# Layer 2 of a two-layer cross-attention kernel: both halves' scores placed around the value products, with a third set of probabilities

## The chip, the core and the metric

The kernel runs on one core of a Trainium2 chip, as one program. The metric is the time of one execution on the device in microseconds (us). The core's engines work in parallel, each through its own queue in order: TensorE (PE in the profile; its weight loads are PEld), VectorE (DVE), ScalarE (ACT), GpSimd (POOL) and SyncE (SP), which only issues DMAs here. ScalarE's queue issues some DMAs as well (ACTq). They wait for one another by semaphores. PSUM holds what TensorE computes until VectorE or ScalarE has read it.

## What is computed

Two cross-attention layers follow each other over 16 batches of 256 positions and 320 channels, with 20 heads of 16 channels. A context of 256 tokens gives keys and values. The changed code is in the second layer; cut to what matters:

```python
scores_t = jnp.einsum('bhsd,bhtd->bhst', q, k_t) * attn_scale
probs_t = jax.nn.softmax(scores_t, axis=-1)
text_out = jnp.einsum('bhst,bhtd->bhsd', probs_t, v_t)
attn_scores = jnp.einsum('bhsd,bhnd->bhsn', q, k_ip) * attn_scale
qsem = jnp.einsum('bhst,bte->bhse', probs_t, text_ehs)
qsem = _l2norm(qsem)
sem = jnp.einsum('bhse,bne->bhsn', qsem, ip_n)
probs_ip = jax.nn.softmax(attn_scores + SEM_SCALE * sem, axis=-1) * spatial_mask
out = (text_out + probs_ip @ v_ip) @ W_out + b_out + residual
```

So each group of four heads needs scores, probabilities, the products of the probabilities with the values, and a quadratic form of the probabilities with the context's Gram matrix, which gives the norm of `qsem`.

## The kernel before

Matrix products that need full accuracy are made of a rounded high part and a low part of each operand. Layer 1 runs in slots 0 to 79 and layer 2 in slots 80 to 159, one slot for a group of four heads, five groups for a batch (`NS` = 80, `NG` = 5). Two more slots finish the last groups. The PE's order is the program's order; on the other engines a scheduler orders the instructions when the program is built, within the dependences and a few chains set by hand (`anchor`, `queued`). Between the parts of a slot, `fill` issues steps of other tasks whose due time has come: projections, keys, the Gram matrix, the image softmax, the output layer.

A slot `k` of layer 2 (`slot1`) consists of these parts:

- `both1(k, t)` for the two halves t = 0 and 1 of the tokens. It makes the transposed scores T of group k (four matmuls, 50 rows each, two row halves of the array at a time), then the scores S of group k + 2 (four matmuls of 48 rows), from which only the row maxima are taken. VectorE reduces S (line 797); ScalarE takes the exponential of T into the probabilities `P` (line 802, two instructions per half). T has two PSUM banks, S has one buffer of two banks.
- `attend1(k - 2)`: eight matmuls of probabilities with values into 32-column quarters of the array (line 843), and four with a constant `zone`, which put the sums `W` of the quadratic form beside them (line 845); `settle1` then transposes and divides on VectorE (lines 889 to 893). The profile counts each of these matmuls twice.
- `norm1(k - 1, u, n)`: seven full-array matmuls for each of two pairs of heads u, in two pieces of four and three (line 830). Each piece's result is multiplied by the rest of the probabilities on VectorE (line 833); then the two pieces are added (line 835, on GpSimd for u = 0 and on VectorE for u = 1). The results lie in PSUM banks X, of which there are three for everything.
- `rounded1(k, u)`: ScalarE rounds half the probabilities (line 820) and GpSimd subtracts that from the probabilities (line 821).
- `stacks(k + 4)`: DMAs that load the stacked queries and keys of a later group into a half of one of the pairs `qs[i]`, `ks[i]`. There are `NR` = 4 such pairs, all used whole in layer 1; in layer 2 they form a ring of eight halves.
- `maxima1(k + 2)`: the maxima are transposed (line 808), cast by ScalarE (line 810) and sent by two DMAs from ScalarE's queue (line 812) into the stack of queries.

The probabilities `P` are two tiles per group out of a ring of `NP` = 4, so two groups' worth.

The tasks that the prediction meets: key-mask products for the image keys (line 501) and a transpose of their scores (978) on VectorE; the keys' high and low parts (147 on ScalarE, 148 on VectorE); the attended rows of the output layer (952 on VectorE, 751 on ScalarE, 753 on VectorE); the values (470 on ScalarE); and the output layer's products (523).

Of the kernel before, what the change touches and what calls it, by code (L numbers as in the profile page):

```python
# [8 lines left out]
F32 = mybir.dt.float32  # L9
FR = mybir.dt.float32r  # L10
# [6 lines left out]
B = 16  # L17
S = 256
# [18 lines left out]
SIZES = dict(RAW=2, KST=2, NP=4, NR=4, CTA=2, CTB=2, WB=4, M=2)  # L37
NS = B * NG
# [3 lines left out]
def RAMP(t):  # L42
    return t if t < -5 or t > 3 else (t + 5) * 0.375
# [5 lines left out]
def xattn2(  # L49
# [28 lines left out]
    f = lambda ap: ap.bitcast(F32)  # L78
    mm = nc.tensor.matmul

    def dma(out, in_):
        nc.sync.dma_start(*(f(ap) if ap.dtype == FR else ap for ap in (out, in_)))
# [4 lines left out]
    sb = ctx.enter_context(tc.tile_pool(name="sb", bufs=2))  # L87

    def bank(tag="X"):
        return ps.tile([128, 512], F32, tag=tag, name=tag, bufs=BANKS[tag])  # L90

    def scores():

        return ps.tile([128, 1024], F32, tag="S", name="S", bufs=1).rearrange("p (h t) -> p h t", h=4)
# [4 lines left out]
    def buf(tag, shape, dtype=F32, bufs=1, name=None):  # L99
        if tag in ("wB", "wD", "vr", "raw"):  # L100
            return sb.tile(shape, dtype, tag=tag, name=name or tag, bufs=bufs)
        size = 1
        for d in shape[1:]:
            size *= d
        if tag not in slots:
            slots[tag] = [0, dtype] + [const_tile([128, max(size, words.get(tag, 0))], f"{tag}_{i}", dtype) for i in range(bufs)]
        n, kind, *ring = slots[tag]
        assert kind == dtype and len(ring) == bufs, tag
        slots[tag][0] += 1
        t = ring[n % bufs][: shape[0], :size]  # L110
        names = "abcd"[: len(shape) - 1]
        if len(names) > 1:
            t = t.rearrange(f"p ({' '.join(names)}) -> p {' '.join(names)}", **dict(zip(names, shape[1:])))
        return t

    def const_tile(shape, tag, dtype=F32):
        return const.tile(shape, dtype, tag=tag, name=tag)
# [23 lines left out]
    def anchor(inst):  # L141
        anchors[inst.ins.engine] = inst
        return inst
# [111 lines left out]
    wq, wo = [lambda s, k, m=slice(None): wqt[:, s, k, m]], []  # L255


    qs = [const_tile([128, 4, S], f"qs{i}", FR) for i in range(SIZES["NR"])]
    ks = [const_tile([128, 4, S], f"ks{i}", FR) for i in range(SIZES["NR"])]
    ind0 = buf("raw", [128, 512], bufs=SIZES["RAW"], name="ind0")[:2, :S]  # L260
    dma(ind0, ind0_d)
    ind0r = buf("mt", [8, S], FR, name="ind0r")[:2]
# [277 lines left out]
    def stack_rows(d):  # L540
        return d.rearrange("r (d h) t -> (r d) h t", h=HP)
# [65 lines left out]
    QK, P, W, R = {}, {}, {}, {}  # L607
# [20 lines left out]

    def stacks1(k):
        b, g = divmod(k - NS, NG)  # L630
        n = 2 * SIZES["NR"]
        i = ((NS - SIZES["NR"]) % SIZES["NR"]) * 2 + (k - NS) % n
        Q, K = QK[k] = [x[i // 2 % SIZES["NR"]][:, 2 * (i % 2) : 2 * (i % 2) + 2] for x in (qs, ks)]
        get("k1", b)
        qd = get("o1", b)[0]
        for u in range(2):
            rows = slice(64 * u, 64 * u + XROW)
            hs = slice(4 * g + u, 4 * g + u + 3, 2)
            if k - NS < n:
                dma(K[64 * u + XROW : 64 * u + KS1], w1["ind"])  # L640
            dma(K[rows], stack_rows(kd[1][b][:, :, 0])[:, hs])
            dma(Q[rows], stack_rows(qd)[:, hs])
# [41 lines left out]
    def attend0(k):  # L684
        b, g = divmod(k, NG)
        v, pv = get("v0", b), bank("P")
        for vt in range(3):
            values0(k, pv, v, vt)
        settle0(b, g, pv)
# [20 lines left out]
    def values0(k, pv, v, vt):  # L710
        t, o = ((0, 0), (0, S), (1, S))[vt]
        for s in range(4):
            h = V0W * (4 * (k % NG) + s)
            mm(  # L714
                pv[32 * s : 32 * s + 32, o : o + S],
                v[:, vt, h : h + 32],
                P[k, s // 2][:, t, s % 2],
                start=vt < 2,
                stop=vt != 1,
            )  # L720
# [56 lines left out]
    def both1(k, t):  # L777

        a = k + 2 < 2 * NS and QK[k + 2] 
        c = NS <= k < 2 * NS and QK[k]  # L780
        if a:
            if t == 0:
                maxes[k + 2] = buf("mn", [128, 4, 4], FR, bufs=2)[:, :2]
            sp = scores()
        if c:
            st = [bank("T").rearrange("p (h t) -> p h t", h=2) for u in range(2)]
            lo = (0, DUP)[t]
            for j in range(2):
                for u in range(2):
                    rows = slice(64 * u, 64 * u + KS1)  # L790
                    mm(st[u][:, j], c[1][rows, j, lo : lo + 128], c[0][rows, j], start=True, stop=True)  # L791
        if a:
            for j in range(2):
                for u in range(2):
                    rows = slice(64 * u, 64 * u + XROW)
                    mm(sp[:, 2 * u + j], a[0][rows, j, t * 128 : (t + 1) * 128], a[1][rows, j], start=True, stop=True)  # L796
            anchor(nc.vector.tensor_reduce(maxes[k + 2][:, t], sp[:, :, :T1], axis=AX.X, op=ALU.max))  # L797
        if c:
            for u in range(2):
                if t == 0:  # L800
                    P[k, u] = buf("P", [128, 2, 2, S], bufs=SIZES["NP"])
                anchor(nc.scalar.activation(P[k, u][:, t], st[u], AF.Exp, scale=SCALE))  # L802

    def maxima1(k):
# [43 lines left out]
    def slot1(k):  # L848
        last = k - 1 if NS < k <= 2 * NS else None
        mine = k < 2 * NS  # L850
        if k == NS:
            yield lambda: maxima(k + 1)
        elif k == NS + 1:
            yield lambda: attend0(k - 2)
        else:
            yield lambda: attend1(k - 2)
        yield lambda: both1(k, 0)
        if last:
            yield lambda: norm1(last, 0, 0)
        yield 0.33  # L860
        if last:
            yield lambda: norm1(last, 0, 1)
        yield lambda: both1(k, 1)
        if mine:
            yield lambda: rounded1(k, 0)
        yield lambda: stacks(k + LEAD)
        if last:
            yield lambda: norm1(last, 1, 0)
        yield 0.67
        if last:  # L870
            yield lambda: norm1(last, 1, 1)
        if mine:
            yield lambda: rounded1(k, 1)
        yield lambda: maxima(k + 2)
        yield 1.0
# [81 lines left out]
    def close0(b):  # L957

        def rows(p, hp):
            nc.vector.transpose(hp, hsn[:, p].rearrange("p f r d -> p (f r d)"))  # L960

        x1 = yield from finish(0, b, resid0.pop() if b == 0 else load(xT_d[b], "xc"), rows)
        dma(x1d[b].rearrange("(k p) t -> p k t", p=128), x1)
# [21 lines left out]
    def task(key, times, make, *needs):  # L985
        tasks[key] = [times, 0, make, needs, len(tasks)]
# [14 lines left out]
    def get(*key):  # L1001
        while key not in results:
            step(key)
        return results[key]
# [20 lines left out]
    def shifted(n, *times):  # L1025

        return [RAMP(n + t) for t in times]
# [10 lines left out]
    for c in range(B // 2):  # L1038
        n, k = 10 * c, [("k0", c)] if c else []
        task(("k0", c), FIRST["k0"] if c == 1 else shifted(n, -14.4, -13.3, -13, -12.4, -12, -10.8, -10.4, -9.8, -9.4, -8.8, -8.4), (lambda c=c: keys0(c)) if c else first_keys,  # L1040
             *([("w4", 0)] if c > 1 else []))
        task(("q0", 2 * c), shifted(n, -11.8, -11, -10, -9, -8), lambda b=2 * c: queries0(b))
        task(("q0", 2 * c + 1), shifted(n, -4.4, -4, -3, -2.8, -2), lambda b=2 * c + 1: queries0(b))
        task(("m0t", 2 * c), shifted(n, -7.4), lambda b=2 * c: tokens0(b), *k)
        task(("m0t", 2 * c + 1), shifted(n, -4.8), lambda b=2 * c + 1: tokens0(b), *k)
        task(("v0", 2 * c), shifted(n, -7, -5.4, -5), lambda b=2 * c: values0_(b), *k)
        task(("v0", 2 * c + 1), shifted(n, -4, -3.8, -3.4), lambda b=2 * c + 1: values0_(b), *k)
        for b, t in ((2 * c, (-7.4, -6.4, -6, -5.4, -5, -4.4, -3.4)), (2 * c + 1, (-2.4, -1.4, -1, -0.8, -0.4, 0, 1.2))):
            task(("s0", b), FIRST["s0"] if b == 1 else shifted(n, *t), lambda b=b: semantic0(b), ("q0", b), ("m0t", b))
            task(("c0", b), shifted(5 * b, *((5.6, 6, 6.6, 7.2, 7.6, 8.2) if b % 2 == 0 else (5.6, 6, 6.6, 7.2, 8.2, 9.2) if b < B - 1 else (6.33, 6.67, 7, 7.67, 8, 8.67))), lambda b=b: close0(b), ("w4", 0))  # L1050
    for b in range(B):
        n = NS + 5 * b
        task(("k1", b), shifted(n, -7, -6.67, -6.33, -5.67, -5, -4.67), lambda b=b: keys1(b), ("w2",), *([("t1", b - 1)] if b else []), *([("w4", 1)] if b > 2 else []))
# [162 lines left out]
```

## Time and profile before

| | |
|---|---|
| time, median of 3 runs | 1549.0 us (1548.74 to 1551.88) |
| the profiled execution's own time | 1545.33 us |
| its span, first to last instruction | 1543.5 us |
| granted TensorE clock | 0.992 |
| mean of one: reduction of S (797), exponential (802), rounding (820) | 1200, 598, 632 ns |
| mean of one: subtraction on GpSimd (821), multiplication (833) | 1321, 679 ns |

The profile gives for each engine its busy time, the groups of instructions, and for each group the idle time ahead of it with what ended it. A timeline row has the start in us from the span's start, the duration, the engine, the line of the kernel, the operation, what is written and read, the shape, and how many such instructions follow each other; in brackets stands the idle time before it and who ended it. Matmuls overlap, so what a part of TensorE's work costs is read from the start of one group to the start of the next. A view of one line lists for how long its engine sat idle before it and until which other line. In a row of windows, the columns are the stretch, its length, then busy time and count of instructions for PE, PEld, DVE, ACT and POOL, the clock, the share of DMA and its rate.

### The profile page before, as it was taken

How to read it: one execution, taken by the hardware profiler on the slowest of the kernel's cores; microseconds unless marked ns; L12 is line 12 of the kernel's file. 1: busy time of each engine (PE TensorE's matmuls, PEld its weight loads, DVE VectorE, ACT ScalarE, POOL GpSimd, SP SyncE). 2: the span in 40 equal slices, each digit the busy share in tenths (PEclk: the TensorE clock that was granted, in tenths of full speed). 3: DMA queues.
4: the chain of work that ended last, by engine and by line, in shares of the span. 5: the costliest groups of instructions: out<-in, count | busy, mean ns of one | idle time of the engine just before them, and what ended most of it. 6: DMA issues, size and time to landing. Idle time of an engine off the chain costs nothing.

```text
span 1543.5 us, 35120 instructions
## 1 busy us (share of the span) xinstructions
PE 1484.2 (96%) x12666; PEld 1202.0 (78%) x12666; DVE 1198.2 (78%) x2468; ACT 949.2 (61%) x2071; POOL 1165.0 (75%) x1178
## 2 busy tenths in 40 slices
PE   7899999999999998899999999999999999999997
PEld 6778888888888887777777787777777777777765
DVE  5457676777676779868888888888888888888796
ACT  5557676767676766755555655655555556556553
POOL 3459797979797867996777877877777777677685
PEclk9999999999999999999999999999999999999999
DMA  6756666656565565654433444344243434432301
GB/s 215 181 164 173 161 178 165 174 160 186 148 193 150 159 185 155 165 163 137 133 124 91 132 125 130 95 129 139 86 128 114 139 97 131 126 117 84 106 26 57
DMA packets 206426, 213.11 MB, mean 138 GB/s; under 512 B 29162, under 2 KB 190156, under 8 KB 206252
## 3 DMA queue, kind: packets, MB, share of 16 engines
q1 hardware_dynamic: 204512, 209.56, 47.3%
q8 instruction: 101, 1.65, 0.5%
q10 hardware_dynamic: 1740, 1.30, 0.3%
q14 instruction: 73, 0.60, 0.1%
HBM read 121.21 MB, written 88.18 MB: 136 GB/s over the span
## 4 chain that ended last, share of the span: by engine, by line
PE 85%; DVE 6%; DMA 3%; POOL 2%; issue 2%; ACT 2%; SPq 0%; ACTq 0%; POOLq 0%; DVEq 0%
PE X L205 23%; PE X L830 17%; PE X L523 11%; PE P L714 7%; PE S L653 6%; PE T L676 4%; PE T L791 4%; PE P L843 4%; PE P L845 3%; PE S L796 2%; PE X L951 1%; PE X L572 1%; DVE wt L835 1%; POOL P L682 1%; PE X L661 1%
## 5 line engine op out<-in xcount | busy, mean ns | idle before, releaser
L821 POOL TENSOR_TENSOR wt<-P,ctb 128x512 f32<-128x512 f32 x320 | 417.8, 1321 | 128.6 <-ACT ctb L820 128.4
L682 POOL TENSOR_TENSOR P<-P,rs 128x512 f32<-128x512 f32 x320 | 413.5, 1316 | 116.6 <-ACT P L679 116.6
L830 PE MATMUL X<-ctb,gm 128*128 128x512 f32 x1120 | 330.3, 413 | 0.9 <-DVE wt L833 0.9
L802 ACT ACTIVATE P<-T 128x512 f32<-128x512 f32 x320 | 174.1, 598 | 105.5 <-PE T L791 104.6
L679 ACT ACTIVATE P<-T 128x512 f32<-128x512 f32 x320 | 174.8, 593 | 97.6 <-PE T L676 73.5
L820 ACT ACTIVATE ctb<-P 128x512 fp32r<-128x512 f32 x320 | 195.4, 632 | 61.7 <-PE X L830 61.3
L830 PEld LDWEIGHTS X<-ctb,gm 128*128 128x128 f32 x1120 | 189.4, 188 | 46.6 <-DVE wt L833 1.5
L797 DVE TENSOR_REDUCE mn<-S 128x4 fp32r<-128x1008 f32 x160 | 192.0, 1200 | 0.2 <-PE S L796 0.2
L833 DVE TENSOR_TENSOR wt<-X,wt 128x512 f32<-128x512 f32 x240 | 161.8, 679 | 11.1 <-PE X L830 10.9
L655 DVE TENSOR_REDUCE mn<-S 128x4 fp32r<-128x716 f32 x160 | 142.5, 891 | 0.0
L714 PE MATMUL P<-P,vr 128*32 128x256 f32 x1920 | 124.6, 389 | 2.5 <-POOL P L682 1.2
L653 PE MATMUL S<-ks,qs 125*128 125x256 f32 x640 | 114.8, 302 | 4.2 <-DVE mn L655 4.2
L523 PE MATMUL X<-hq,wE 128*128 128x256 f32 x768 | 110.3, 287 | 6.8 <-ACT hq L512 4.0
L653 PEld LDWEIGHTS S<-ks,qs 125*128 125x128 f32 x640 | 86.5, 190 | 36.9 <-issue 30.4
L523 PEld LDWEIGHTS X<-hq,wE 128*128 128x128 f32 x768 | 102.8, 194 | 10.8 <-ACT hq L512 4.5
L523 PE MATMUL X<-ho,wF 128*128 128x256 f32 x768 | 108.8, 285 | 0.7 <-DVE ho L753 0.6
L205 PE MATMUL X<-cta,wA 128*128 128x252 f32 (+1 forms) x720 | 99.8, 284 | 8.5 <-ACT wA L147 5.7
L835 POOL TENSOR_TENSOR wt<-wt 128x512 f32<-128x512 f32 x80 | 103.6, 1296 | 2.5 <-DVE wt L833 2.5
L676 PE MATMUL T<-qs,ks 127*128 127x256 f32 x640 | 104.7, 286 | 0.0
L523 PEld LDWEIGHTS X<-ho,wF 128*128 128x128 f32 x768 | 100.8, 190 | 4.6 <-DVE ho L753 1.1
L205 PEld LDWEIGHTS X<-cta,wA 128*128 128x128 f32 x720 | 92.5, 192 | 11.5 <-ACT wA L147 5.9
L791 PEld LDWEIGHTS T<-qs,ks 50*128 50x128 f32 x640 | 47.7, 184 | 61.7 <-issue 33.2
(203 smaller groups left out, 3008.4 us busy)
## 6 DMA issues: line engine op xcount, KB each, us to landing
qd<-q SPq DMA_DIRECT2D x96, 384.0 KB
kd<-kst SPq DMA_DIRECT2D x73, 256.0 KB
rawc<-in_cT_dram SPq DMA_DIRECT2D x60, 256.0 KB
qs<-qd SPq DMA_DIRECT2D x80, 192.0 KB
ks<-kd SPq DMA_DIRECT2D x80, 192.0 KB
ks<-kd SPq DMA_DIRECT2D x160, 96.0 KB
qs<-qd SPq DMA_DIRECT2D x160, 96.0 KB
kd<-kst SPq DMA_DIRECT2D x21, 512.0 KB
```

Of the source, the lines that this page charges most:

```text
L205: last = mm(out, lhs(a, k), rhs(b, k), start=i == 0, stop=i == len(terms) - 1)
L523: mm(pp, w(s, k, slice(m * 128, (m + 1) * 128)), a[:, t], start=i == 0, stop=i == len(terms) - 1)
L653: mm(sp[:, h], Q[: XROW + T0, h, t * 128 : (t + 1) * 128], K[: XROW + T0, h], start=True, stop=True)
L676: mm(st[p][:, j], K[:KS0, 2 * p + j, t * 128 : (t + 1) * 128], Q[:KS0, 2 * p + j], start=True, stop=True)
L679: exp = anchor(nc.scalar.activation(pt, st[p], AF.Exp, scale=SCALE))
L682: anchor(nc.gpsimd.tensor_mul(pt, pt, rs[:, t : t + 1].to_broadcast([128, 2, S])))
L714: mm(pv[32 * s : 32 * s + 32, o : o + S], v[:, vt, h : h + 32], P[k, s // 2][:, t, s % 2], start=vt < 2, stop=vt != 1,)
L797: anchor(nc.vector.tensor_reduce(maxes[k + 2][:, t], sp[:, :, :T1], axis=AX.X, op=ALU.max))
L802: anchor(nc.scalar.activation(P[k, u][:, t], st[u], AF.Exp, scale=SCALE))
L820: nc.scalar.activation(R[k, u][:, t], P[k, u][:, t], AF.Copy, scale=0.5)
L821: anchor(nc.gpsimd.tensor_sub(W[k, u][:, t], P[k, u][:, t], f(R[k, u][:, t])))
L830: mm(yp, gm[:, gb], R[k, u][:, kt], start=i == 0, stop=i == len(blocks[n]) - 1)
```

## The change

In `slot1`, the two halves of `both1` are put around `attend1`, and all four pieces of `norm1` come after them. `attend0` of layer 1's last group runs one slot earlier, between the halves of slot 80. Since the first half of group k now writes probabilities before `attend1(k - 2)` has read its own, three sets of `P` are needed: the fourth pair of stacks becomes a pair of tiles in another pool (tags `qsl`, `ksl`), which layer 1 uses as stacks and layer 2 as the probabilities of every third group. The ring of stacks in layer 2 thus has six halves. The due times of the last batch's layer-1 output are earlier. The text has one line more above these functions, so that line 797 becomes 798 and so on.

```diff
-    qs = [const_tile([128, 4, S], f"qs{i}", FR) for i in range(SIZES["NR"])]
-    ks = [const_tile([128, 4, S], f"ks{i}", FR) for i in range(SIZES["NR"])]
+    last_stack = lambda shape, dtype, u: sb.tile(shape, dtype, tag=("qsl", "ksl")[u], name=("qsl", "ksl")[u], bufs=1)
+    qs = [const_tile([128, 4, S], f"qs{i}", FR) for i in range(SIZES["NR"] - 1)] + [last_stack([128, 4, S], FR, 0)]
+    ks = [const_tile([128, 4, S], f"ks{i}", FR) for i in range(SIZES["NR"] - 1)] + [last_stack([128, 4, S], FR, 1)]
...
-        n = 2 * SIZES["NR"]
-        i = ((NS - SIZES["NR"]) % SIZES["NR"]) * 2 + (k - NS) % n
-        Q, K = QK[k] = [x[i // 2 % SIZES["NR"]][:, 2 * (i % 2) : 2 * (i % 2) + 2] for x in (qs, ks)]
+        n = 2 * (SIZES["NR"] - 1)
+        i = (k - NS) % n
+        Q, K = QK[k] = [x[i // 2][:, 2 * (i % 2) : 2 * (i % 2) + 2] for x in (qs, ks)]
...
-                    P[k, u] = buf("P", [128, 2, 2, S], bufs=SIZES["NP"])
+                    P[k, u] = buf("P", [128, 2, 2, S], bufs=SIZES["NP"]) if (k - NS) % 3 else last_stack([128, 2, 2, S], F32, u)
...
         if k == NS:
             yield lambda: maxima(k + 1)
-        elif k == NS + 1:
-            yield lambda: attend0(k - 2)
-        else:
+        yield lambda: both1(k, 0)
+        if k == NS:
+            yield lambda: attend0(k - 1)
+        if k > NS + 1:
             yield lambda: attend1(k - 2)
-        yield lambda: both1(k, 0)
+        yield lambda: both1(k, 1)
         if last:
             yield lambda: norm1(last, 0, 0)
         yield 0.33
         if last:
             yield lambda: norm1(last, 0, 1)
-        yield lambda: both1(k, 1)
         if mine:
             yield lambda: rounded1(k, 0)
         yield lambda: stacks(k + LEAD)
```

More of the change, by code (lines that the diff above doesn't have):

```diff
@@ L1049, in xattn2 @@
             task(("s0", b), FIRST["s0"] if b == 1 else shifted(n, *t), lambda b=b: semantic0(b), ("q0", b), ("m0t", b))
-            task(("c0", b), shifted(5 * b, *((5.6, 6, 6.6, 7.2, 7.6, 8.2) if b % 2 == 0 else (5.6, 6, 6.6, 7.2, 8.2, 9.2) if b < B - 1 else (6.33, 6.67, 7, 7.67, 8, 8.67))), lambda b=b: close0(b), ("w4", 0))
+            task(("c0", b), shifted(5 * b, *((5.6, 6, 6.6, 7.2, 7.6, 8.2) if b % 2 == 0 else (5.6, 6, 6.6, 7.2, 8.2, 9.2) if b < B - 1 else (5.67, 6, 6.33, 7, 7.67, 8))), lambda b=b: close0(b), ("w4", 0))
     for b in range(B):
```

## The prediction, made before the changed kernel was run

> **What bounds the kernel now.** I read the page first, then the windows of layer 2, the waits of the zone products, and the timeline of one whole batch.
>
> ```profile
> span 1543.5 us, 35120 instructions
> PE 1484.2 (96%) x12666; PEld 1202.0 (78%) x12666; DVE 1198.2 (78%) x2468; ACT 949.2 (61%) x2071; POOL 1165.0 (75%) x1178
> ```
> ```profile
> 833.00:886.00 53.00, 52.47 (x430) 40.59 (x427) 44.70 (x84) 30.39 (x67) 40.02 (x44) 1.00 0.41 126
> ```
> ```profile
>   DVE wt L835: 23.5, 38
> ```
>
> TensorE has no slack: in one batch of layer 2 (five slots, 53 us) it is busy for 52.47 us, VectorE for 44.70, GpSimd for 40.02. The last row, from the view of line 845 over 780 to 1470 us, gives almost all the idle time that there is: the zone products wait 23.5 us for VectorE's sum (line 835). So time is won or lost on TensorE alone: by its own instructions, by changes of the array's shape, and by waits in its fixed order.
>
> I number a batch's slots 1 to 5 by their starts in the trace: 949.32, 959.30, 970.39, 979.77, 990.30. I count each slot 13 or 14 times: 16 batches, less the first two and the last, where the neighbouring work differs. Slot 2 shows the lengths:
>
> ```profile
> 959.30 1.07 PE L843 MATMUL P<-P,v1t 128*32 128x256 f32 x16
> 959.57 1.09 DVE L501 TENSOR_TENSOR kb<-kip,kmask 128x384 fp32r<-128x384 f32 x1
> 960.19 0.61 PE L845 MATMUL P<-wt,zone 128*32 128x256 f32 x8
> 960.73 0.50 PE L791 MATMUL T<-qs,ks 50*128 50x256 f32 x4
> 960.95 1.26 DVE L501 TENSOR_TENSOR kb<-kip,kmask 128x384 fp32r<-128x384 f32 x1
> 961.07 0.40 PE L796 MATMUL S<-ks,qs 48*128 48x256 f32 x4
> 961.27 1.09 ACT L802 ACTIVATE P<-T 128x512 f32<-128x512 f32 x2 [2.08 <-PE T L791]
> 961.40 1.20 PE L830 MATMUL X<-ctb,gm 128*128 128x512 f32 x4
> 963.06 1.20 DVE L797 TENSOR_REDUCE mn<-S 128x4 fp32r<-128x1008 f32 x1
> ...
> 964.21 0.86 PE L830 MATMUL X<-ctb,gm 128*128 128x512 f32 x3
> 964.99 0.51 PE L791 MATMUL T<-qs,ks 50*128 50x256 f32 x4
> 965.66 1.20 PE L830 MATMUL X<-ctb,gm 128*128 128x512 f32 x4
> 966.70 1.12 PE L523 MATMUL X<-ho,wF 128*128 128x256 f32 x8
> 967.66 0.86 PE L830 MATMUL X<-ctb,gm 128*128 128x512 f32 x3
> 968.36 0.28 PE L808 MATMUL X<-ident_r,mn 128*4 128x128 f32 x2
> ```
>
> From start to start: values 0.89, zone 0.54, T 0.34, S 0.33; front of a slot 2.10. The second T and S take 0.67 (964.99 to 965.66). Three norm products ahead of other full-array work take 0.70 (967.66 to 968.36) and ahead of T 0.78, so full to half rows costs 0.08. Four of them behind S take 1.04 where 4/3 of 0.70 is 0.93, so half rows to full costs 0.11. Both halves and the attend part thus take 2.10 + 0.67 + 0.08 + 0.11 = 2.96 us of an unstalled slot. The exponentials begin 0.54 after T and end 1.63 after it.
>
> **The change, part by part.** *Order.* TensorE gets the same instructions; T, S, attend, T, S, then full-array work. One full-to-rows and one rows-to-full change and the change into the value columns go; one into T's rows and one from rows to columns come. The last is not in the trace: 0 if the array takes it for nothing, 0.2 if it is twice the others; I take 0.10, the nearest rows' size. Unstalled, the front is 0.34 + 0.33 + 0.10 + 0.89 + 0.54 + 0.34 + 0.33 = 2.87, so 0.09 is saved per slot (from 0.19 saved to 0.01 lost).
>
> *New closeness.* S has one buffer, T two banks. The second S waits for the first reduction (line 797), the second T for the first two exponentials (802). They had the first half's norm products and a fill between them, 3.6 us in slot 2 (961.40 to 964.99); now only the 1.4 us of attend. From the slot's start T's second bank is wanted at about 2.3 and S at 2.54. So the reduction must start by 1.3 and the exponentials by 1.2. Whatever those engines do first at a slot's start is on the path. In the changed program as built, the first reduction stands in VectorE's queue behind these tails:
>
> *Slot 2.* Sum (835), both key-mask products (501) with a transpose between, then the reduction. The second 501 ends at 962.21, 2.91 after the start. Reduction to 4.11, second S to 4.44, norm products then, against 2.96: **+1.48**, 13 times, +19.2. Before, the reduction began even later (963.06), but the S that needs it came at 965.33 (964.99 + 0.34) and nothing showed.
>
> ```profile
> L501 DVE TENSOR_TENSOR kb<-kip,kmask x32: 535/1182/1422, 604.7 to 1387.4; 128x384 fp32r<-128x384 f32 x32
> ```
> A 501 takes 0.54 to 1.42 us. If both fell to 0.54 the slot would cost 1.2 less; if both took 1.42, 0.5 more. I keep the slot's own two: the subtractions beside them stay, slightly later. The Trainium skill, "SBUF — State Buffer", section "Who interferes with whom", has a VectorE instruction with two SBUF inputs contend with a GpSimd one that reads SBUF, the later one held until the first ends. By that rule at its full size each 501 could wait out a 1.3 us subtraction, 1.84 each and +1.3 for the slot; no row here is over 1.42, so the rows decide.
>
> *Slot 4.*
>
> ```profile
> 979.77 1.07 PE L843 MATMUL P<-P,v1t 128*32 128x256 f32 x16
> 980.66 0.59 PE L845 MATMUL P<-wt,zone 128*32 128x256 f32 x2
> 981.05 0.68 DVE L835 TENSOR_TENSOR wt<-wt,X 128x512 f32<-128x512 f32 x1
> 981.78 0.63 PE L845 MATMUL P<-wt,zone 128*32 128x256 f32 x6 [0.53 <-DVE wt L835]
> 982.35 0.50 PE L791 MATMUL T<-qs,ks 50*128 50x256 f32 x4
> 983.01 1.20 PE L830 MATMUL X<-ctb,gm 128*128 128x512 f32 x4
> ```
> The sum ends 1.96 after the start (the chain from the last norm product, which stays). The zone wait of 1.14 is now largely covered by T and S, but the reduction follows at 1.96 to 3.16; with 0.05 for the signal (981.73 to 981.78) the second S ends at 3.54. Before 3.24 + 0.86 = 4.10: **-0.56**, 14 times, -7.8.
>
> *Slot 5.*
>
> ```profile
> 990.30 1.07 PE L843 MATMUL P<-P,v1t 128*32 128x256 f32 x16
> 990.46 0.35 ACT L810 CAST mt<-X 4x256 fp32r<-4x256 f32 x1
> 990.83 1.29 ACTq L812 DMA_DIRECT2D qs<-mt  x2
> 991.74 0.42 DVE L952 TENSOR_TENSOR X<-hT,X 128x256 f32<-128x256 f32 x1
> 992.10 0.51 PE L791 MATMUL T<-qs,ks 50*128 50x256 f32 x4
> 992.19 0.37 ACT L751 CAST ho<-X 128x256 fp32r<-128x256 f32 x1 [1.12 <-DVE X L952]
> 992.63 1.09 ACT L802 ACTIVATE P<-T 128x512 f32<-128x512 f32 x2
> 992.77 1.21 PE L830 MATMUL X<-ctb,gm 128*128 128x512 f32 x4
> ```
> ScalarE issues the two maxima DMAs (1.29 us) and casts `ho` once VectorE has its sum (952, done 1.86 after the start). In the built order the exponentials stand behind both, as before, but T now runs at the start. If nothing shifts they run from 2.26 to 3.35; the second T ends at 3.66, S at 3.99. The first `ho` cast (0.37) now precedes the maxima's cast, which can push the DMAs to 2.18 and all of it to 4.30. Before 2.47 + 0.86 = 3.33: +0.66 to +0.97; I take **+0.80**, 14 times, +11.2. Were ScalarE not in the way, VectorE's order alone (952, then the reduction: 1.86 to 3.06, S to 3.44) gives +0.11; with another 0.4 from casts ahead, +1.4.
>
> *Slots 3 and 1.*
>
> ```profile
> 970.39 1.07 PE L843 MATMUL P<-P,v1t 128*32 128x256 f32 x16
> 970.50 0.53 ACT L470 ACTIVATE v1t<-X,tmask 128x320 f32<-128x320 f32 x1 [0.71 <-PE X L205]
> ```
> ```profile
> 949.32 1.07 PE L843 MATMUL P<-P,v1t 128*32 128x256 f32 x16
> 949.83 0.42 DVE L148 TENSOR_TENSOR kst<-X,kst 128x252 fp32r<-128x252 f32 x1 [0.77 <-ACT kst L147]
> ```
> Slot 3: the reduction now stands ahead of the small softmax steps, but ScalarE has a DMA issue (0.65) and the value copy (0.53) before the exponentials: they end near 2.3, so -0.09 to +0.3, taken **+0.10**, 13 times, +1.3. Slot 1: VectorE is free at 0.93, in time: **-0.09**, 13 times, -1.2.
>
> *GpSimd, queues, buffers.*
>
> ```profile
> 956.31 1.30 POOL L835 TENSOR_TENSOR wt<-wt 128x512 f32<-128x512 f32 x1
> ```
> In some slots GpSimd's sum now follows two subtractions, not one. It ended at 957.61 for a zone product at 960.19; 1.3 later, with the zone 0.77 later, is still in time. The norm products now run as seven in a row on three banks, but the fill before them and the multiplications (0.7 each) free a bank in time once the second reduction is done. Stack loads keep their place behind the fill, on SP's queue too; their ring of six halves is rewritten two slots after its last reader instead of four, covered by some 20 us. Four indicator DMAs fewer: nothing. The third set of probabilities is what allows the order and costs no instruction.
>
> *Sum.* 19.2 - 7.8 + 11.2 + 1.3 - 1.2 = +22.7 us in 67 of 80 groups; the first and last ones, waiting and unwaiting on the same engines, 0 (-4 to +4). Profiled execution 1545.3 + 22.7 = 1568; it lies 3.7 under the median of 1549.0, so **1572**.
>
> **The rivals.**
> *VectorE alone* (chance 0.15): ScalarE gets its exponentials out in time. Slots 3 and 5 fall to -0.09 and +0.11: 19.2 - 7.8 + 1.5 - 1.2 - 1.2 = +10.5, **1559**. For it: the exponentials start 0.54 after T in slots 2 and 5; against it: T was then 1.4 us into the slot.
>
> *Faster* (0.14): the zone wait is covered and the second half waits for nothing. It decides if the reduction starts by 1.3 in every slot. Slot 4 then gains 0.67 and slot 5 its wait of 0.36 (992.10 against 990.30 + 1.43), 14 times, 14.4, and 0.09 in 80 slots, 7.2: **1527**. For it: 23.5 us of waits are there. Against: the built order of slot 2.
>
> *Worse* (0.10): contention and ScalarE at their upper ends: 13 x 0.5 + 14 x 0.6 + 13 x 0.2 = 17.5 more, **1589**.
>
> *Only a move* (0.03): waits leave the zone products and appear at S in equal size, within 0.2% of 1549. Slot 2, which has no wait now, speaks against.
>
> **How the numbers follow.** The forecast has 0.58, with 1560 to 1585 of its own. Slower by over 0.2% (3 us, about what this kernel's measurement can tell) are it, VectorE alone and worse: 0.83; faster 0.14; same 0.03. The range 1553 to 1590 holds these slower cases with their bounds and leaves the faster one out.
>
> **What would show it.** Right: in slot 2 about 1.6 us of TensorE idle before the second S, released by line 797's reduction (one line further down in the changed text); in slot 5 about 1 us before the second T, released by the exponentials; the zone waits under 10 us in all; slots 2 and 5 longer, slot 4 shorter. Wrong: the second S starting within 2.6 us of the first T in slot 2, or 501 moved behind the reduction; a wait on GpSimd or on the X banks as the largest one.

## The result, and the profile after

The changed kernel takes 1557.1 us (median of 5 runs, 1554.9 to 1560.7) against 1549.0 for the kernel before on the same chip (5 runs, 1548.5 to 1551.9): ratio 1.0046, 95% interval 1.003 to 1.0061. It is slower, by 8 us, where 23 were forecast. Its profiled execution took 1554.9 us, 9.6 more than that of before; the terms of the prediction are held against these 9.6.

First the page of the changed kernel, then its windows over one batch (slots 5, 1, 2, 3, 4; columns as before: PE, PEld, DVE, ACT, POOL busy, clock, DMA share, GB/s), then what kept the engine idle ahead of the zone products from 780 to 1470 us (us, times).

```profile
span 1553.1 us, 35232 instructions
PE 1470.1 (95%) x12666; PEld 1209.7 (78%) x12666; DVE 1200.6 (77%) x2468; ACT 951.6 (61%) x2071; POOL 1167.4 (75%) x1178
```
```profile
944.16:998.35 54.19, 51.73 (x429) 41.06 (x428) 45.18 (x84) 30.65 (x67) 40.19 (x44) 1.00 0.38 117
```
```profile
  DVE wt L836: 4.6, 13
```

TensorE does the same 12666 instructions and is busy for 0.74 us less in a batch (51.73 against 52.47), yet the batch is 1.2 us longer. So the change saved TensorE time in its own work and in the zone wait (4.6 us against 23.5), and lost more in new waits. A view of one line adds the idle time of weight loads (PEld) and of matmuls (PE), which overlap, so the 23.5 counts part of the wait twice: the weight loads of the kernel before have 16.3 of it (first row below). The view of waits over 780 to 1470 us names the waits of each engine (engine, tile and line that waited, what released it; us in total, times, longest); the other two rows are the changed kernel's new ones:

```profile
PEld P L845 <- DVE wt L835: 16.3, 25, 1.3
```
```profile
PEld S L797 <- DVE mn L798: 19.5, 24, 1.4
PEld X L952 <- ACT mt L811: 17.1, 12, 1.4
```

The first of these two was forecast, the second was not. Slot by slot, I take the start of each slot's first norm product in both traces, and how far the changed kernel lags there. One batch:

| slot | before | after | lag | change in this slot |
|---|---|---|---|---|
| 1 | 951.43 | 958.43 | 7.00 | |
| 2 | 961.40 | 969.61 | 8.21 | +1.21 |
| 3 | 972.50 | 980.48 | 7.98 | -0.23 |
| 4 | 983.01 | 990.50 | 7.49 | -0.49 |
| 5 | 992.77 | 1001.13 | 8.36 | +0.87 |
| 1 | 1004.49 | 1012.63 | 8.14 | -0.22 |

The same over all 13 batches between 755 and 1446 us, beside the sum on record (which counts slots 4 and 5 once more):

| | slot 2 | slot 3 | slot 4 | slot 5 | slot 1 | first groups | last groups | sum |
|---|---|---|---|---|---|---|---|---|
| predicted | +19.2 | +1.3 | -7.8 | +11.2 | -1.2 | 0 | 0 | +22.7 |
| measured | +15.5 | -3.0 | -7.1 | +10.9 | -4.5 | +3.4 | -5.7 | +9.5 |

Slot 2 in the changed kernel's timeline (965.39 is its first T):

```profile
965.39 0.51 PE L792 MATMUL T<-qs,ks 50*128 50x256 f32 x4
965.71 0.59 DVE L502 TENSOR_TENSOR kb<-kip,kmask 128x384 fp32r<-128x384 f32 x1
966.31 2.82 POOL L822 TENSOR_TENSOR wt<-P,ctb 128x512 f32<-128x512 f32 x2
966.59 1.42 DVE L502 TENSOR_TENSOR kb<-kip,kmask 128x384 fp32r<-128x384 f32 x1
967.50 0.50 PE L792 MATMUL T<-qs,ks 50*128 50x256 f32 x4
967.93 1.20 DVE L798 TENSOR_REDUCE mn<-S 128x4 fp32r<-128x1008 f32 x1
969.18 0.50 PE L797 MATMUL S<-ks,qs 48*128 48x256 f32 x4 [1.18 <-DVE mn L798]
969.61 1.20 PE L831 MATMUL X<-ctb,gm 128*128 128x512 f32 x4
```

This is the forecast chain: both key-mask products, then the reduction, then the second S, released by it. Only the two products are shorter than assumed, 2.01 us together and not 2.35. The second of them lies beside a GpSimd subtraction (822). An unstalled front (slot 1) shows the lengths:

```profile
955.64 0.51 PE L792 MATMUL T<-qs,ks 50*128 50x256 f32 x4
955.99 0.41 PE L797 MATMUL S<-ks,qs 48*128 48x256 f32 x4
956.33 1.07 PE L844 MATMUL P<-P,v1t 128*32 128x256 f32 x16
957.22 0.61 PE L846 MATMUL P<-wt,zone 128*32 128x256 f32 x8
957.76 0.51 PE L792 MATMUL T<-qs,ks 50*128 50x256 f32 x4
958.43 1.19 PE L831 MATMUL X<-ctb,gm 128*128 128x512 f32 x4
```

The values start 0.34 after S, where S ahead of other work takes 0.33: going from rows to columns costs nothing that can be seen. The front is 2.79, where 2.87 was assumed and 2.96 stood before. And the end of slot 4, with slot 5's start:

```profile
941.13 1.05 PE L831 MATMUL X<-ctb,gm 128*128 128x512 f32 x3
941.81 1.15 ACT L821 ACTIVATE ctb<-P 128x512 fp32r<-128x512 f32 x2 [0.89 <-POOL wt L822]
942.87 0.35 ACT L752 CAST ho<-X 128x256 fp32r<-128x256 f32 x1
943.12 0.36 ACT L811 CAST mt<-X 4x256 fp32r<-4x256 f32 x1
943.53 0.30 PEld L952 LDWEIGHTS X<-rs,rs 128*128 128x128 f32 x2 [1.42 <-ACT mt L811]
943.53 0.70 PE L952 MATMUL X<-rs,rs 128*128 128x256 f32 x2 [1.23 <-DMA out_dram<-xc]
944.16 0.50 PE L792 MATMUL T<-qs,ks 50*128 50x256 f32 x4
945.13 0.60 ACT L803 ACTIVATE qsl<-T 128x512 f32<-128x512 f32 x1
```

The second image-value product (952) idles 1.23 us and starts at 943.53, 0.05 after the maxima's cast (811) ends at 943.48; its own row names an output DMA, but the row of its weight load names that cast, in all 12 batches that have the wait. As the changed program is built, this product's PSUM bank is the one that the maxima's small products have just left, in these 12 batches; in the program before it was one left by T. ScalarE comes to the cast late, behind two probability casts (821) and the output cast (752). The two probability casts had themselves waited 0.89 us. Their row names a GpSimd subtraction (822); but as the program is built they overwrite the tile that the slot's last norm product (831) reads, the subtractions of that tile are a slot older, and the casts start 0.67 to 0.69 us behind that product's start in all 12 batches. So the queue ahead of the maxima's cast is tied to the last norm product. Slot 5's front then has no stall: its exponentials run at 945.13, 0.97 after T.

### The profile page after: what moved, and what is told of

It is laid out like the page before. It is cut to its first block, busy times and chain, and to the rows that moved or that the text cites. A ratio compares the mean times of both kernels' runs of the same rounds, so it can differ in the third digit from the quotient of the medians.

```text
span 1553.1 us, 35232 instructions
## 1 busy us (share of the span) xinstructions
PE 1470.1 (95%) x12666; PEld 1209.7 (78%) x12666; DVE 1200.6 (77%) x2468; ACT 951.6 (61%) x2071; POOL 1167.4 (75%) x1178
## 4 chain that ended last, share of the span: by engine, by line
PE 74%; POOL 8%; DVE 8%; DMA 4%; ACT 3%; issue 2%; SPq 1%; ACTq 0%; POOLq 0%; DVEq 0%
PE X L205 21%; PE X L831 13%; PE X L524 10%; PE P L715 6%; PE S L654 5%; PE T L677 4%; POOL wt L822 3%; PE P L844 3%; PE T L792 3%; PE S L797 2%; POOL P L683 2%; DMA out_dram<-xc 2%; DVE mn L798 2%; DVE kb L502 2%; PE P L846 1%
## 5 line engine op out<-in xcount | busy, mean ns | idle before, releaser
L822 POOL TENSOR_TENSOR wt<-P,ctb 128x512 f32<-128x512 f32 x212 | 274.6, 1315 | 107.5 <-ACT ctb L821 107.5
L831 PE MATMUL X<-ctb,gm 128*128 128x512 f32 x1120 | 308.8, 405 | 0.0
L680 ACT ACTIVATE P<-T 128x512 f32<-128x512 f32 x320 | 174.7, 593 | 99.1 <-PE T L677 74.4
L831 PEld LDWEIGHTS X<-ctb,gm 128*128 128x128 f32 x1120 | 196.2, 189 | 41.0 <-issue 0.4
L821 ACT ACTIVATE ctb<-P 128x512 fp32r<-128x512 f32 x212 | 123.5, 625 | 57.1 <-PE X L831 48.0
L803 ACT ACTIVATE P<-T 128x512 f32<-128x512 f32 x212 | 114.5, 594 | 45.4 <-PE T L792 44.4
L822 POOL TENSOR_TENSOR wt<-qsl,ctb 128x512 f32<-128x512 f32 x54 | 70.9, 1324 | 50.8 <-ACT ctb L821 50.8
L726 DVE STREAM_TRANSPOSE nt<-P 128x512 f32<-128x512 f32 x80 | 57.1, 713 | 49.1 <-PE P L715 49.0
L655 DVE TENSOR_REDUCE mn<-S 128x4 fp32r<-128x308 f32 x160 | 74.8, 467 | 23.9 <-PE S L654 23.6
L654 PE MATMUL S<-ks,qs 125*128 125x256 f32 x480 | 86.3, 303 | 3.3 <-DVE mn L656 3.3
```

Of the source, the lines that this page charges most:

```text
L654: mm(sp[:, h], Q[: XROW + T0, h, t * 128 : (t + 1) * 128], K[: XROW + T0, h], start=True, stop=True)
L680: exp = anchor(nc.scalar.activation(pt, st[p], AF.Exp, scale=SCALE))
L821: nc.scalar.activation(R[k, u][:, t], P[k, u][:, t], AF.Copy, scale=0.5)
L822: anchor(nc.gpsimd.tensor_sub(W[k, u][:, t], P[k, u][:, t], f(R[k, u][:, t])))
L831: mm(yp, gm[:, gb], R[k, u][:, kt], start=i == 0, stop=i == len(blocks[n]) - 1)
```

## The experiments

All times are medians; ratios are to the kernel before, run on the same chip. Rows of experiment kernels carry their own line numbers, up to six higher. A few kernels below lost some 7 us twice in layer 1, which their edits do not touch, in some or most executions (the last section shows where, in the traces); where that is so, I compare slots of layer 2.

**The key mask out of slot 2's way.**

```diff
-        qh, qd = yield from queries(1, xs)
-
-        kb = image1(b)
-        yield
+        parts = queries(1, xs)
+        next(parts)
+        yield
+        next(parts)
+        kb = image1(b)
+        yield
+        qh, qd = yield from parts
+        yield
...
-            nc.vector.tensor_mul(
+            queued(nc.vector.tensor_mul(
```

> The changed kernel with one thing moved: the two products of the key mask (501 and 502 in the changed kernel's numbering) are issued one and a half slots earlier and behind slot 5's second reduction on VectorE, so that they no longer stand ahead of slot 2's first reduction. Theory (VectorE's queue is what stalls slot 2): slot 2's front falls from 4.19 to about 2.8 us and its second S follows its second T at once; 13 batches by 1.4 give -18, so 1557 becomes about 1539; slot 5 gets 1.1 to 2.5 us of VectorE before its first norm product is taken and may give up to 4 us of it back (1543). Rival (another wait stands right behind the reduction in slot 2, the exponentials or GpSimd's sum): the front of slot 2 stays above 3.5 us and the time above 1550.

Measured 1539.6, ratio 0.9944 (0.9928 to 0.996): faster than both kernels. Slot 2 in its timeline, and the 26 mask products from 780 to 1470 us (ns min/median/max):

```profile
960.25 0.50 PE L792 MATMUL T<-qs,ks 50*128 50x256 f32 x4
961.04 1.21 DVE L798 TENSOR_REDUCE mn<-S 128x4 fp32r<-128x1008 f32 x1
962.36 0.51 PE L792 MATMUL T<-qs,ks 50*128 50x256 f32 x4
963.03 0.96 PE L831 MATMUL X<-ctb,gm 128*128 128x512 f32 x3
```
```profile
L502 DVE TENSOR_TENSOR kb<-kip,kmask x26: 543/549/568, 785.1 to 1419.0; 128x384 fp32r<-128x384 f32 x26
```

The reduction starts 0.79 after T, the front is 2.78, and each slot 2 is 1.40 to 1.45 shorter, as the theory had it; the rival falls. Slot 5 gives nothing back: at their new place the products take 0.55 each. In the changed kernel the first of each pair takes 0.57 to 0.59 and the second 1.42, and all the second ones run beside a GpSimd subtraction; at the new place no GpSimd instruction runs beside them but one short copy.

**The second image-value product and its bank.** Three edits bear on it, in this order below: the first two products in the halves of one bank (e5); the output cast of the first product (`last_ho`) held behind the maxima's (f2, on e1_mask); the maxima ahead of the last norm product and of the casts that wait for it (f1, on e1_mask).

```diff
-            hp = bank()[:, :S]
+            if not (l and p == 1):
+                pair = bank()
+            hp = pair[:, S:] if l and p == 1 else pair[:, :S]
...
-        nc.scalar.copy(mt[:, 0], mp[:4, :S])
+        cast = nc.scalar.copy(mt[:, 0], mp[:4, :S])
+        if last_ho:
+            queued(last_ho.pop(), cast)
...
+        yield lambda: maxima(k + 2)
         if last:
             yield lambda: norm1(last, 1, 1)
         if mine:
             yield lambda: rounded1(k, 1)
-        yield lambda: maxima(k + 2)
```

> The changed kernel with the first two image-value products (952) in the two halves of one PSUM bank, so that the second no longer takes the bank which the maxima have just been cast out of. Theory (the bank is what holds the second product at the end of slot 4 for 1.2 to 1.4 us, and only that): the wait there goes, slot 5 starts 1.4 us earlier, and then the stall that the prediction had for slot 5 appears, ScalarE's two DMA issues and the casts ahead of the exponentials, +0.8 us in slot 5's front: -0.6 by 12 batches = -7, about 1550. Rival 1 (no stall in slot 5 even then): -1.4 by 12 = -17, about 1540. Rival 2 (the wait is ScalarE's late cast, whatever the bank): another instruction of slot 4 or 5 waits as long, 1557 within 2.

Measured 1589.6, ratio 1.0276 (1.0255 to 1.0298): all three expectations missed. The view of waits has a new row, for the same product:

```profile
PEld X L954 <- DVE ho L754: 28.4, 13, 2.2
```

The second half waited until VectorE had read the first half for the last time: in this program the wait goes by the bank, not by the columns. The Trainium skill, "PSUM — Partial Sum Buffer", section "PSUM bank collisions raise a hardware error", asks for that: guard PSUM by bank and quadrant, not by address. The run confirms that the bank's last reader sets this product's start: with VectorE as that reader the wait is up to 2.2 us.

> Base: e1_mask (1539.6). One edit more: ScalarE's output cast (752) of the first image-value product is held behind the maxima's cast of the same slot. Theory (the wait at the end of slot 4 is for the bank that the maxima's cast frees, and so as long as ScalarE's queue ahead of that cast): the second image-value product starts 0.35 us earlier, one cast's time: -4, about 1535. Rival (the output cast, now behind the two DMA issues of 1.3 us, comes between slot 5's exponentials and holds them by what was gained or more): 1540 or above.

Measured 1537.3, ratio 0.9937 (0.9921 to 0.9954). In the traces the product comes 0.26 earlier in each batch than in e1_mask, slot 5 keeps its length: the theory, with 0.26 in place of 0.35.

> Base: the changed kernel with the key-mask products moved as in e1_mask (1539.6). One edit more: the maxima's two small products, their cast and their two DMAs are issued ahead of the slot's last norm product and of the second pair of probability casts, not behind them. Theory (at the end of slot 4 the second image-value product waits for the maxima's cast because ScalarE comes to it after two probability casts and the output cast): the cast runs about 1 us earlier and the wait of 1.2 to 1.4 us goes; the DMA issues too are over before slot 5's exponentials, so nothing comes back there: -1.4 by 12 = -17, about 1523. Rival 1 (the stall goes to slot 5's front, as the prediction had it, 0.8 us): -7, about 1532. Rival 2 (the maxima, put ahead, delay the last norm product or the sums behind it as much): 1540 within 3.

Measured 1534.4 (four executions, 1528.3 to 1552.1; the longest is the one in the trace, with the loss in layer 1, and the ratio is without it), ratio 0.9904 (0.9879 to 0.9929). Slot 4 falls from 11.43 to 9.93 us, slot 5 grows from 11.48 to 12.20: net -0.8 per batch, rival 1 in size. Its timeline at that place:

```profile
954.04 0.36 ACT L811 CAST mt<-X 4x256 fp32r<-4x256 f32 x1 [0.71 <-PE X L809]
954.60 0.59 PE L952 MATMUL X<-rs,rs 128*128 128x256 f32 x2
955.12 0.50 PE L792 MATMUL T<-qs,ks 50*128 50x256 f32 x4
956.43 0.58 ACT L803 ACTIVATE qsl<-T 128x512 f32<-128x512 f32 x1
956.83 1.19 DVE L798 TENSOR_REDUCE mn<-S 128x4 fp32r<-128x1008 f32 x1
957.52 0.50 PE L792 MATMUL T<-qs,ks 50*128 50x256 f32 x4
958.08 0.50 PE L797 MATMUL S<-ks,qs 48*128 48x256 f32 x4
```

The bank, still the maxima's, is free in time. Now slot 5 waits at its front, 0.6 us, and two things are late there: ScalarE's exponentials and VectorE's reduction.

**What makes slot 5 late.** One more edit each: the maxima's DMAs issued by SyncE (g1), the second pair of probability casts issued in the next slot behind its first exponentials (g2), both (g3).

```diff
-            nc.scalar.dma_start(
+            nc.sync.dma_start(
...
-        if mine:
-            yield lambda: rounded1(k, 1)
         yield 1.0
...
         yield lambda: both1(k, 0)
+        if last:
+            yield lambda: rounded1(last, 1)
```

> Base: f1_max_first (1533 to 1534), in which slot 5's front is 0.6 us longer than an undisturbed one. One edit more: the maxima's two DMAs are issued by SyncE instead of ScalarE. Theory (the DMA issues, 0.63 us each on ScalarE, are what is late ahead of slot 5's exponentials): the stall shrinks by up to the one issue that still stands behind the output cast there, 0.3 to 0.6 by 13 = -4 to -8, about 1527. Rival (what is late are the probability casts and the output cast that waits for VectorE): within 2 of 1533.

> Base: f1_max_first (1533 to 1534). One edit more: the second pair of probability casts of a slot, with its two GpSimd differences, is issued in the next slot, behind the exponentials of that slot's first half. Theory (those two casts of 0.55 us stand ahead of slot 5's exponentials and make the second T late): slot 5's front falls from 3.39 to about 2.8: -0.6 by 13 = -8, about 1526. Rival (GpSimd then gets its differences 2 us later, in every slot, and the products with the zone or the norm products of the slot wait for it): 1540 or above.

> Base: g2_late_round, and the maxima's DMAs issued by SyncE as in g1_max_first_sp. Theory (both stand ahead of the exponentials, and their costs add): 2 to 8 us below g2_late_round. Rival (only one of the two was on the path): within 2 us of the lower of g1_max_first_sp and g2_late_round, or of both.

Measured 1547.9, 1546.3 and 1547.0, ratios 0.9996 (0.997 to 1.0022), 0.9992 (0.9968 to 1.0015) and 1.0002 (0.999 to 1.0014). g1's profiled execution, without the loss in layer 1, took 1533.1, g3's, with it, 1550.8, and most executions of all three lie nearer the second, so these medians decide nothing for or against the theories. In the profiled slots, slot 4 lasts 9.92 in each and slot 5 lasts 12.30, 12.08 and 12.28, against f1_max_first's 9.93 and 12.20. From g3's timeline of slot 5:

```profile
954.86 0.50 PE L792 MATMUL T<-qs,ks 50*128 50x256 f32 x4
955.69 0.59 ACT L803 ACTIVATE qsl<-T 128x512 f32<-128x512 f32 x1
955.71 0.42 DVE L953 TENSOR_TENSOR X<-hT,X 128x256 f32<-128x256 f32 x1
956.04 0.68 DVE L836 TENSOR_TENSOR wt<-wt,X 128x512 f32<-128x512 f32 x1
956.64 1.20 DVE L798 TENSOR_REDUCE mn<-S 128x4 fp32r<-128x1008 f32 x1
957.89 0.50 PE L797 MATMUL S<-ks,qs 48*128 48x256 f32 x4
```

The exponentials start 0.83 after T, 0.48 earlier than in f1_max_first, and the slot is no shorter: the second S still waits for the reduction, which VectorE starts 1.78 after T, behind the image values' sum (953) and the zone sum (836). So taking ScalarE's work away gains nothing, and the trace names VectorE; no run moved its two sums.

**The norm product between the halves.** The first edit is to the changed kernel, the second run adds the DMAs on SyncE.

```diff
-        yield lambda: both1(k, 1)
         if last:
             yield lambda: norm1(last, 0, 0)
+        yield lambda: both1(k, 1)
```

> The changed kernel with one part of the order undone: the first norm product stands between the two halves' scores again, behind the values, and not behind the second half. Theory (the front's length is set by the reduction's time and by the array's switches): the product's 1.0 us covers most of slot 2's wait for the reduction (from 1.33 to about 0.3 us), the fronts without a stall go from 2.78 back to about 2.96; here the second image-value product has another bank, so the 1.2 us at the end of slot 4 go too: -13 for slot 2, +11 for the switches, -7 to -17 for the bank: 1540 to 1550. Rival (which of the two stands last does not matter, the changed kernel loses by the values' late start): 1557 within 3.

> Base: e3_norm_between (1560.7), where the second image-value product has another bank and does not wait, and slot 5 is 2.2 us longer than in the changed kernel. One edit more: the maxima's two DMAs are issued by SyncE, not by ScalarE. Theory (what the prediction had for slot 5: two DMA issues of 0.65 us and the output cast stand ahead of the exponentials on ScalarE): the exponentials of slot 5 start up to 1.3 us earlier, the late first S and zone products of slot 5 go, and the probability casts behind them come earlier: -1.2 to -2 by 13 = -15 to -25, about 1541. Rival (SyncE waits in its queue for loads, so the maxima rows come late and the scores behind them wait): 1560 or above. Rival 2 (slot 5 is held by the casts and sums behind the second half, not by the DMAs): 1555 to 1562.

Measured 1560.7 and 1560.7, ratios 1.0088 (1.0067 to 1.011) and 1.009 (1.0073 to 1.0107): 3.6 above the changed kernel and so nearer e3's rival, though its slots move as the theory has it. Slots 1 and 3 grow by 0.2, the two changes of shape come back; slot 2 falls from 12.31 to 11.31; slot 4, where the bank is another, falls from 11.43 to 9.85; and slot 5 grows from 11.48 to 13.73, in e3 and f4 alike. Two rows of e3's waits make up most of it: the first S and a norm product in slot 5.

```profile
PEld X L831 <- DVE wt L834: 16.6, 12, 1.4
PEld S L797 <- ACT mt L811: 6.8, 13, 0.5
```

So where the second product does not wait, slot 5 does; f4's rival 2 holds: moving the DMAs off ScalarE brings slot 5's exponentials from 2.41 after its first T to 0.67 and saves nothing. (1560.7 is also at the edge of f4's first rival, late maxima rows, but no wait of TensorE for these DMAs stands in its view.)

**What is not the order's.**

> Everything of the change but the order of layer 2's groups: the fourth stack pair as third set of probabilities, the ring of six half stacks and the last batch's due times, with the old order of slots. Theory (those parts cost nothing by themselves, and all of the +8 us is the order's): 1549 within 3 us of the kernel before. Rival (the smaller ring of stacks holds loads up, or the third set of probabilities frees ScalarE earlier): over 3 us away from it, upwards for the ring, downwards for the set.

Measured 1551.6, ratio 1.0014 (0.9998 to 1.003): the steady part of layer 2 is that of before, 53.13 against 53.23 us per batch, so the smaller ring and the third set of probabilities cost nothing there. But layer 2 starts late, as in the changed kernel: its first norm product comes 5.6 us later than in the kernel before, the changed kernel's 4.9. f3_start moves the last layer-1 group's values back into layer 2's second slot (on e1), h1_old_due gives the changed kernel the old due times, h2_new_due gives the kernel before the new ones (the diff shows f3's edit and h2's; h1's is h2's reversed; h2's lines are cut to the part that changes).

```diff
-        if k == NS:
-            yield lambda: attend0(k - 1)
+        if k == NS + 1:
+            yield lambda: attend0(k - 2)
...
-else (6.33, 6.67, 7, 7.67, 8, 8.67)
+else (5.67, 6, 6.33, 7, 7.67, 8)
```

> Base: e1_mask (1539.6). One edit more: the last layer-1 group's values stand in layer 2's second slot again, between that slot's two halves, and not in the first slot. Theory (layer 2's start lost 4.9 us because nothing stands between the second slot's two halves, so the second half waits 2.9 us for VectorE, which itself waits for the mask's DMA): the values cover about 0.9 us of products and the wait falls by as much or more: -1 to -4, about 1537. Rival (VectorE gets the transpose and the sums of that group in the very slot where it is late): 1540 or above.

> The changed kernel with one part undone: the last batch's layer-1 output projection keeps its old due times. The changed kernel's first norm product of layer 2's third slot comes 4.9 us later than in the kernel before, and e4_old_order, with the old order of slots, has the same delay (5.6). Theory (the delay is the due times': the earlier projection pieces stand ahead of the last layer-1 group on VectorE and ScalarE): it goes, about 1557 - 4.9 = 1552. Rival 1 (it is the ring of six half stacks or the third set of probabilities): 1557 within 2, the delay stays. Rival 2 (the earlier due times pay for themselves later, by an earlier load of batch 15): slower than 1557.

> The kernel before with the last batch's new due times alone. Theory (the due times alone bring the delay of 5 us at the start of layer 2): 1553 to 1554. Rival (the delay comes from the ring or the third set of probabilities): 1548 to 1549, as before.

f3_start took 1542.4, ratio 0.9962 (0.9945 to 0.9978), not better than e1_mask: the rival. h2_new_due took 1549.1, ratio 1.0013 (1.0001 to 1.0025). The first zone products of layer 2 in the kernel before, in h2_new_due and in h1_old_due:

```profile
706.99 0.59 PE L845 MATMUL P<-wt,zone 128*32 128x256 f32 x2
```
```profile
701.29 3.19 PE L205 MATMUL X<-wC,cta 128*128 128x320 f32 x12 [2.76 <-DVE tmp L731]
713.00 0.61 PE L845 MATMUL P<-wt,zone 128*32 128x256 f32 x8
```
```profile
709.95 0.61 PE L846 MATMUL P<-wt,zone 128*32 128x256 f32 x8
```

The due times alone bring a start 6.0 us late, 2.8 of them one fill product that waits for VectorE's last layer-1 values. In the changed kernel they make the start 3.2 us later (713.19 against 709.95) and the end 3.4 us shorter; the profiled spans are equal, 1553.1 and 1553.7. So the late start was the due times', as both theories said, but their times are off: h2_new_due was to take 1553 to 1554 and is nearer the rival's 1548 to 1549, and h1_old_due, which was to fall to 1552, came out as its rival 2 said, slower than 1557. In the changed kernel the due times give the start back at the end. (h1_old_due's median is 1567.2, ratio 1.0115 (1.0084 to 1.0147): the profiled execution took 1555.5, the other three over 1565, and no profile shows why.)

> e1_mask (1539.6) with the last batch's old due times. Theory (the two parts are separate: the key mask's place costs slot 2 its 1.4 us per batch, the due times the start): 1535 to 1540, by what h1_old_due shows at the start. Rival (one depends on the other through the banks' placement): outside of that.

> f2_cast_first (1537.3: the key mask moved, the output cast behind the maxima's cast) with the last batch's old due times, to see whether the three corrections add up: 1537 less what h1_old_due gains at the start, 1532 to 1537, and so 12 to 17 below the kernel before. Rival (the corrections take from each other): 1540 or above.

Measured 1550.8, ratio 1.0015 (0.9992 to 1.0038), and 1547.4, ratio 1.0001 (0.9989 to 1.0013): both above what the theories said. Layer 2's steady batches are those of e1_mask and f2_cast_first (52.78 against 52.81, and 52.48 against 52.52 us); h4's profiled execution lost 15 us in layer 1, h3's had no such loss and took 1534.4, 13 and more below its others. Whether the corrections add up in a whole execution these two leave open.

## Why the prediction was right and wrong

The direction was right and the size was not: +22.7 us on record, +9.5 in the profiled executions (8 in the medians). What failed is the sum. Its largest mis-sized terms are those of slots 3 and 1: on record +0.1 us together, measured -7.5 (the switch from rows to columns, priced at 0.10 us, measured 0.01; ScalarE's work in slot 3, priced at 0.19, held nothing up). Slot 2 was right in mechanism and 3.7 us too dear, and slot 5's step was wrong in mechanism, with the right size by luck.

- **TensorE bounds the kernel, and the order decides by its waits.** Right: same instructions, a longer batch, and e4_old_order without the order has the old batch. The 23.5 us of zone waits, the case for *Faster*, were nearer 16, as said above.
- **Slot 2, +1.48 by the key mask ahead of the reduction.** Right in mechanism, shown by e1_mask; the size was 1.20. The two products took 2.01 us and not 2.35 (-0.34), which is nearly all by which the reduction comes earlier (2.54 after the first T and not 2.91); their lengths were taken over from the slot of before, where GpSimd's subtractions ran beside both, and now one runs beside the second alone.
- **Slot 4, -0.56.** Right: -0.54. The zone wait is covered, the reduction follows, no more.
- **Slot 5, +0.80 by ScalarE's DMA issues and casts ahead of the exponentials.** The size is right (+0.84) by luck, the step is wrong. The price falls at slot 4's end, where a PSUM bank is freed late by the maxima's cast; f2_cast_first and f1_max_first show it by moving that cast. "Free a bank in time" was the error: it counted three banks, and did not look at which bank each product is given, who reads that bank last, and what that engine's queue waits for. With that wait out of the way (f1_max_first) slot 5 does stall, 0.6, and then at VectorE's reduction: g1 to g3 and f4 take ScalarE's DMAs and casts away, and the slot 5 of the traces gains 0.12 us at most. The rival "VectorE alone" had that mechanism (reduction behind 952), at +0.11; in f1_max_first slot 5's first norm product follows slot 4's 9.76 us behind, against 9.67 in the kernel before, so +0.09.
- **Slots 3 and 1, +0.10 and -0.09.** Too dear: both came out at -0.2. The switch from rows to columns was priced at 0.10 as its neighbours are, and costs nothing; slot 3's value copy and DMA issue on ScalarE, priced at 0.19, made nothing late. This is 7.6 of the 13 us by which the sum was too high: 2.6 the switch, 2.5 ScalarE in slot 3, 1.9 two stalls of 0.95 us that the profiled execution of before happened to have in slots 1, and the rest unexplained. Slot 2 is 3.7 and the ends 2.3.
- **First and last groups, 0 (-4 to +4).** -2.3, as +3.4 and -5.7; the due times, which I did not price, move time from one to the other.
- **GpSimd's sum in time, the ring of six halves free.** Right: no row of GpSimd is among TensorE's waits after the change, and e4_old_order has the old batch.

The likeliest case was thus right in direction and in slots 2 and 4, wrong in how slot 5 loses, and about two and a half times too high. The named signs were mixed: slot 2's wait and the zone waits came as said (5 us, under 10); slot 5's did not, and a wait on an X bank is the second largest, close behind (17.1 against 19.5 us of weight loads).

## What to carry to other kernels

Before costing a reordered step, write down for each engine what now stands ahead of the instruction that frees its buffer, and what that engine itself waits for, and check which PSUM bank the built program gives each product: a bank handed on within a slot is a hidden queue position. A wait that is taken away shows the next one behind it; price a slot by its second latest engine too. Rare set-up work that a queue runs "whenever its buffer is free" belongs behind the reduction that TensorE waits for: moving two instructions took the changed order from a ratio of 1.0046 to 0.9944.

## What the runs showed of the hardware

One VectorE instruction of 128x256 elements (line 515, two SBUF inputs and a column of constants) takes 0.47 us in the median and in the changed kernel 1.42 at most. In h4_mask_cast_old_due it took 7.07, with GpSimd running without a gap beside it, and TensorE sat idle for 5.2 us until a VectorE reduction behind it (579):

```profile
141.65 7.07 DVE L515 SCALAR_TENSOR_TENSOR hq<-hq,tmask,xq 128x256 fp32r<-128x256 f32 x1
150.35 1.19 PE L654 MATMUL S<-ksl,qsl 125*128 125x256 f32 x4 [5.20 <-DVE mx L579]
```
```profile
139.33 5.03 POOL L683 TENSOR_TENSOR P<-P,rs 128x512 f32<-128x512 f32 x4
144.32 1.26 POOL L514 TENSOR_TENSOR hq<-xq,hq 128x512 fp32r<-128x512 f32 x1
145.55 0.44 POOL L737 TENSOR_TENSOR hsn<-tmp 128x128 f32<-128x128 f32 x1
145.97 2.47 POOL L683 TENSOR_TENSOR P<-P,rs 128x512 f32<-128x512 f32 x2
```

It ends at 148.72, just after GpSimd's unbroken stretch at 148.44. The Trainium skill, "SBUF — State Buffer", section "Who interferes with whom", calls the port pair that the two engines share an exclusive lock, and lets the order of issue decide who blocks; here VectorE was held over some seven GpSimd instructions, not one. Such instructions of 7.07 to 7.08 us stand twice, near 141 and 375 us, in the profiles of f1_max_first, g2, g3 and h4, which fall 6.7 to 8.0 us behind e1_mask at each of the two places. In the other 13 profiles the same line stays at 1.43 or less. That it comes from the two engines' SBUF access is argued from the times; no run changed it alone.
